# Key projection in seven block products from batch 2 on, and a first pass with the norm in halves and the row twice in PSUM

## The chip, the core and the metric

The kernel runs on one core of a Trainium2 chip. The time is that of the whole program on the device, in microseconds (us). TensorE (PE in the profile) multiplies matrices: a weight load (PEld) puts one operand into the array, the other streams through it, and the result goes to PSUM, a small memory of eight banks. VectorE (DVE), ScalarE (ACT) and GpSimd (POOL) do the rest, and SyncE (SP) issues most transfers (DMA). Each engine works through its own queue in order, and waits where an input isn't there yet or a buffer isn't free yet.

## The reference

The input x has 16 batches of 1024 nodes with 256 channels; adj is 1024 x 1024, and everything is float32. Two layers, each added to x:

```
h = relu(layernorm(x))
# layer 0
diff = mean over channels of h: column minus row
A    = 2 * | |sigmoid(diff) - 0.5| - 0.5 |
g    = relu( (h^T @ (adj * A_s)) * para )      A_s: A made symmetric
q    = g^T in 4 heads;   k, v = h @ kv_w
x    = x + softmax(q k^T * scale) @ v
# layer 1
h    = relu(layernorm(x))
agg  = A_hat @ h                               A_hat: adj + 1, normalized by its degrees
x    = x + batchnorm(relu(batchnorm(agg @ W1^T + b1)) @ W2^T + b2)
```

The two batch norms run over all batches and nodes, so that layer 1 ends only after a pass over everything.

## The kernel before

**The stages of a batch.** For each batch b the program records, in this order: `attention(b)`, `graph(b + 1)` and `linear1_all(b)`. Under a manual schedule the engines keep the order in which the instructions are recorded, and tiles take buffers from pools: a new tile takes the buffer that has been free longest, and its first writer waits until the old tile's last reader is done. In PSUM the pool `ps_s` has three buffers of two banks (tag "s"), and `ps_o` and `ps_t` have one bank each.

**`graph(b, between)`** (line 308) multiplies h with the weighted adjacency, chunk by chunk of 128 nodes: per chunk c four products of 128x512, into two PSUM tiles `f_gps`. A table `between` says what the other engines are given ahead of each chunk. Then come the keys (line 343): for each half d of the channels, two column halves g and two input halves e, so eight products of 128x512, in two PSUM tiles `f_kps`, each copied by ACT into kT (line 350). Behind each half DVE multiplies `f_gps` with para into qT (line 352) and ACT applies the ReLU and the scale (line 353). Then come the values (line 358), 16 products of 128x256, in two PSUM tiles `f_vps`, copied by ACT into v (line 365). Keys and values read hT, the transposed h.

**hT** is made by `turn_h` (line 288): DVE transposes blocks of 32 into two tiles `f_hQ` (tag "acc", two buffers), and 32 small transfers (line 302) put them in place; they are issued by POOL, in the first batch by SP.

**`linear1`** (line 550) and `linear1_seven` (line 648) already form their block products with seven instead of eight multiplications: a product of 2x2 blocks is written as seven products of sums of blocks. Four of the seven go into one PSUM tile one after another, and ACT copies what stands in it after each of them.

**Norm.** A `Norm` (line 206) takes statistics of 8 chunks of 128x256 on DVE (lines 221, 223), inverts the root of the variance on POOL (line 227), forms a shift on DVE (line 231), and applies norm and ReLU on ACT (line 236), which also sums each row for the mean over channels.

**The first pass.** Nothing runs beside batch 0's preparation, so its order is written out from line 878 on: the norm of batch 0, with two of the eight turns of adj (`turn_adj`: eight transposes on PE, and a copy into ahatT on ACT or DVE, lines 824 and 825) between its statistics and its activations; two more turns; `prepare_row(0)` (line 258: the column factor on DVE, the row of sums spread over all partitions by eight transposes on PE and copied out by ACT); then `weights` (line 275) per chunk: Abs and Tanh on ACT and a product with adj on DVE. The other turns, the turn of W1, the statistics of batch 1 and the row sums of adj stand in the table of `graph(0)`.

Of the kernel before, what the change touches and what calls it, by code (L numbers as in the profile page):

```python
# [29 lines left out]
def fast_path(  # L30
# [36 lines left out]
    w1s_d = dram.tile([P, 4, FC * P // 2], F32, tag="fw1s", name="fw1s")  # L67
    t_d = [dram.tile([P, 4, 512], F32, tag=f"ft_{k}", name=f"ft_{k}") for k in range(3)]
# [101 lines left out]
    with ExitStack() as stage:  # L170
# [12 lines left out]
        def load_x(b):  # L183
            xt = big.tile([P, NC, C], F32, tag="x", name=f"f_x_{b}")
            nc.sync.dma_start(xt, x[b].rearrange("(c p) d -> p c d", p=P))
            return xt


        xs, xr = {0: load_x(0)}, {}
# [16 lines left out]
        class Norm:  # L206
# [11 lines left out]

            def stats(self, c0, c1):
# [5 lines left out]
            def invert(self):  # L225
                nc.vector.tensor_scalar_add(self.var, self.mv[:, :, 1], EPS)
                nc.gpsimd.tensor_tensor(self.rstd, self.var, mhalf, ALU.pow)

            def relu(self, c0, c1):
                if c0 == 0:  # L230
                    nc.vector.scalar_tensor_tensor(  # L231
                        self.shift, self.mv[:, :, 0], -1.0, self.rstd, ALU.mult, ALU.mult
                    )
                    self.h = two.tile([P, NC, C], F32, tag="h", name=f"f_h_{self.name}")
# [23 lines left out]
        def prepare_row(b):  # L258
# [14 lines left out]
            nc.scalar.copy(row, ps.rearrange("p c q -> p (c q)"))  # L273
# [34 lines left out]
        def graph(b, between):  # L308
# [5 lines left out]
            for c in range(NC):  # L314
                for step in between.get(c, ()):
                    step()
                if c == 5:
                    for d in range(CC):
                        t = w4.tile([P, N], F32, tag="w4", name=f"f_para_{b}_{d}")
                        nc.sync.dma_start(t, para_v[:, d, :])  # L320
                        para_t.append(t)
                w = ws.pop((b, c))
                for d in range(CC):
                    for g in range(NH):
                        nc.tensor.matmul(  # L325
                            gps[d][:, ts(g, 512)],
                            hs[b][:, c, ts(d, P)],
                            w[:, ts(g, 512)],
                            start=(c == 0),
                            stop=(c == NC - 1),  # L330
                        )
# [7 lines left out]
            for d in range(CC):  # L339
                ps = ps_s.tile([P, N], F32, tag="s", name=f"f_kps_{b}_{d}")  # L340
                for g in range(NH):
                    for e in range(CC):
                        nc.tensor.matmul(  # L343
                            ps[:, ts(g, 512)],
                            kvw_t[:, e, ts(d, P)],
                            hT[e][:, ts(g, 512)],
                            start=(e == 0),
                            stop=(e == CC - 1),
                        )
                nc.scalar.copy(kT[:, d, :], ps)  # L350
# [3 lines left out]
            for c4 in range(0, NC, 4):  # L354
                ps = ps_s.tile([P, 4, C], F32, tag="s", name=f"f_vps_{b}_{c4}")
                for i in range(4):
                    for e in range(CC):
                        nc.tensor.matmul(  # L358
                            ps[:, i, :],
                            hT[e][:, ts(c4 + i, P)],  # L360
                            kvw_t[:, e, C : 2 * C],
                            start=(e == 0),
                            stop=(e == CC - 1),
                        )
                nc.scalar.copy(v[:, c4 : c4 + 4, :], ps)
# [276 lines left out]

        def load_w1_sums(b):
# [177 lines left out]
        def turn_adj(i, copy):  # L821
# [1057 lines left out]
```

## Time and profile before

| | us |
|---|---|
| time, median of three runs | 2459.4 (2456.1 to 2460.28) |
| the profiled execution | 2456.69 |
| its span, first to last instruction | 2454.9 |
| PE busy | 2399.2 (98%) |
| DVE busy | 1693.8 (69%) |
| ACT busy | 1319.9 (54%) |
| key products (line 343), all batches | 113.2 |
| value products (line 358), all batches | 113.1 |
| graph products (line 325), all batches | 444.7 |

A line of a group reads: line of the kernel, engine, operation, tile written <- tiles read, shapes, count | busy us, mean ns of one | idle time of that engine just before, and what ended it. A float32 matmul of the program appears as two records. The chain that ended last follows the work back from the last instruction, at each step to what released it; its lines are start, duration (us), and what ran. Times within a trace count from the start of the span.

### The profile page before, as it was taken

Reading aid. Unit: us, or ns where it says so; the run is one execution under the profiler, and the core shown is the slowest. Engines: PE = TensorE matmul, PEld = TensorE weight load, DVE = VectorE, ACT = ScalarE, POOL = GpSimd, SP = SyncE. Lnnn points to the kernel's source line nnn. Section 1 sums busy time; section 2 is a strip of 40 time slices with the busy share of each in tenths; the row PEclk is TensorE's granted clock in tenths of the full one; section 3 lists DMA queues with packets and bytes.
Section 4 is the critical chain, followed back from the end, with each engine's and each line's share of the span. In section 5 each row is a group of like instructions: output and inputs, shape, how many; then the busy total and the mean of one; then the engine's idle time right before and its main releaser. Section 6 shows DMA issues by size and latency. Waiting matters only on the chain.

```text
span 2454.9 us, 24503 instructions
## 1 busy us (share of the span) xinstructions
PE 2399.2 (98%) x8070; PEld 1060.6 (43%) x8070; DVE 1693.8 (69%) x2309; ACT 1319.9 (54%) x1896; POOL 307.8 (13%) x545
## 2 busy tenths in 40 slices
PE   7999999999999999999999999999999999999995
PEld 4443444434343434444343434343444434434444
DVE  4787668584949486776859494957668586747746
ACT  7746546464636455554546364646546465346643
POOL 2030202020020302020201102030202020000000
PEclk9999999999999999999999999999999999999998
DMA  5041414222331414142323223141414211455569
GB/s 180 5 142 61 146 61 124 82 84 71 113 93 60 139 61 146 60 138 69 115 61 105 81 82 115 64 142 61 146 60 122 84 39 57 134 201 171 170 214 371
DMA packets 174424, 271.81 MB, mean 111 GB/s; under 512 B 37585, under 2 KB 121041, under 8 KB 174289
## 3 DMA queue, kind: packets, MB, share of 16 engines
q1 hardware_dynamic: 154128, 237.62, 30.0%
q0 software_dynamic: 15552, 15.77, 2.5%
q10 hardware_dynamic: 4608, 16.78, 1.7%
q8 instruction: 66, 1.08, 0.2%
q14 instruction: 70, 0.57, 0.1%
HBM read 165.68 MB, written 70.84 MB: 96 GB/s over the span
## 4 chain that ended last, share of the span: by engine, by line
PE 94%; DVE 2%; DMA 2%; ACT 1%; issue 1%; POOL 0%; ACTq 0%; SPq 0%; DVEq 0%; POOLq 0%
PE f_s L379 18%; PE f_o L420 18%; PE f_gps L325 17%; PE f_aps L568 15%; PE f_zps L663 6%; PE f_vps L358 5%; PE f_kps L343 4%; PE f_zx L1092 3%; PE f_zm L1092 2%; PE f_z2ps L1030 2%; DVE f_x1t L1358 1%; PE f_zps L744 1%; PE f_zps3b L663 0%; PE f_zps3a L663 0%; ACT f_h_a L236 0%
## 5 line engine op out<-in xcount | busy, mean ns | idle before, releaser
L387 ACT ACTIVATE f_p<-f_s 128x1024 f32<-128x1024 f32 x512 | 477.4, 1046 | 153.4 <-PE f_s L379 153.2
L396 DVE TENSOR_TENSOR f_acc<-f_acc,f_p 128x1024 f32<-128x1024 f32 x384 | 470.4, 1225 | 42.1 <-DVE f_acc L396 1.4
L379 PE MATMUL f_s<-f_qT,f_kT 64*128 64x512 f32 x2048 | 456.9, 596 | 0.0
L420 PE MATMUL f_o<-f_p,f_v 128*64 128x512 f32 x2048 | 453.6, 595 | 0.0
L325 PE MATMUL f_gps<-f_w,f_h_a 128*128 128x512 f32 x1024 | 444.7, 594 | 3.8 <-DVE f_w L283 3.8
L302 POOL DMA_DIRECT2D f_hT<-f_hQ x480 | 235.7, 499 | 1219.1 <-PE f_gps L325 1088.4
L379 PEld LDWEIGHTS f_s<-f_qT,f_kT 64*128 64x128 f32 x2048 | 190.6, 185 | 263.5 <-ACT f_p L387 117.3
L325 PEld LDWEIGHTS f_gps<-f_w,f_h_a 128*128 128x128 f32 x1024 | 192.8, 190 | 251.9 <-issue 228.6
L420 PEld LDWEIGHTS f_o<-f_p,f_v 128*64 128x64 f32 x2048 | 141.4, 137 | 304.4 <-issue 255.6
L283 DVE SCALAR_TENSOR_TENSOR f_w<-f_w,f_adj 128x1024 f32<-128x1024 f32 x128 | 155.0, 1212 | 52.4 <-ACT f_w L282 52.4
L279 ACT ACTIVATE f_w<-f_row,f_col 128x1024 f32<-128x1024 f32 x128 | 148.2, 1157 | 27.2 <-DMA f_row<-frow 22.6
L236 ACT ACTIVATE f_h_b<-f_x,f_shift_b,f_rstd_b 128x256 f32<-128x256 f32 x128 | 64.6, 587 | 158.5 <-DVE f_shift_b L231 158.5
L611 DVE TENSOR_TENSOR f_aggT<-f_u,f_aps 128x512 f32<-128x512 f32 x16 | 11.0, 687 | 185.5 <-PE f_aps L568 185.5
L282 ACT ACTIVATE f_w<-f_w 128x1024 f32<-128x1024 f32 x128 | 135.4, 1058 | 4.1
L568 PE MATMUL f_aps<-f_ahatT,f_hs 128*128 128x512 f32 x256 | 115.1, 592 | 0.0
L343 PE MATMUL f_kps<-f_hT,f_kvw 128*128 128x512 f32 x256 | 113.2, 593 | 1.5 <-DVE f_qT L352 1.5
L568 PE MATMUL f_aps<-f_t,f_hs 128*128 128x512 f32 x256 | 112.5, 592 | 1.5 <-DVE f_hs L562 1.5
L358 PE MATMUL f_vps<-f_kvw,f_hT 128*128 128x256 f32 x512 | 113.1, 379 | 0.0
L568 PE MATMUL f_aps<-f_ahatT,f_h_b 128*128 128x512 f32 x256 | 112.6, 593 | 0.0
L358 PEld LDWEIGHTS f_vps<-f_kvw,f_hT 128*128 128x128 f32 x512 | 97.3, 190 | 20.1 <-issue 6.2
L236 ACT ACTIVATE f_h_a<-f_x,f_shift_a,f_rstd_a 128x256 f32<-128x256 f32 x128 | 75.0, 587 | 54.4 <-DVE f_shift_a L231 54.4
L393 DVE TENSOR_TENSOR f_acc<-f_p,f_p 128x1024 f32<-128x1024 f32 x64 | 76.2, 1191 | 30.7 <-ACT f_p L387 30.7
(187 smaller groups left out, 2554.7 us busy)
## 6 DMA issues: line engine op xcount, KB each, us to landing
f_t<-ft SPq DMA_DIRECT2D x84, 512.0 KB, 7.6
f_x<-in_x_dram SPq DMA_DIRECT2D x32, 1024.0 KB, 5.6
fz<-f_z SPq DMA_DIRECT2D x64, 512.0 KB, 9.4
f_zb<-fz SPq DMA_DIRECT2D x36, 512.0 KB, 4.2
f_para<-in_L_gnn_para_dram SPq DMA_DIRECT2D x32, 512.0 KB, 4.7
f_att<-f_oT SPq DMA_DIRECT2D x512, 32.0 KB, 1.9
fx<-f_x SPq DMA_DIRECT2D x16, 1024.0 KB, 5.9
f_x1t<-fx SPq DMA_DIRECT2D x32, 512.0 KB, 6.3
```

Source lines behind the costliest of these rows:

```text
L279: nc.scalar.activation(w, rows[b], AF.Abs, bias=cols[b][:, c : c + 1], scale=0.5 / C)
L283: nc.vector.scalar_tensor_tensor(w, w, 1.0, adj_t[c], ALU.subtract, ALU.mult)
L302: queue.dma_start(to[ts(k, 32), ts(a, 32 * NC)], t[ts(a, 32), k].rearrange("i c r -> i (c r)"),)
L325: nc.tensor.matmul(gps[d][:, ts(g, 512)], hs[b][:, c, ts(d, P)], w[:, ts(g, 512)], start=(c == 0), stop=(c == NC - 1),)
L343: nc.tensor.matmul(ps[:, ts(g, 512)], kvw_t[:, e, ts(d, P)], hT[e][:, ts(g, 512)], start=(e == 0), stop=(e == CC - 1),)
L358: nc.tensor.matmul(ps[:, i, :], hT[e][:, ts(c4 + i, P)], kvw_t[:, e, C : 2 * C], start=(e == 0), stop=(e == CC - 1),)
L379: nc.tensor.matmul(ps[:, e, :], kT[rows_e, pair, ts(m, P)], qT[rows_e, pair, ts(g, 512)], start=True, stop=True,)
L387: nc.scalar.activation(p, ps, AF.Exp)
L396: nc.vector.tensor_add(acc_of[s], acc_of[s], p)
L420: nc.tensor.matmul(o_of[s][e * HD : (e + 1) * HD, :], v[:, m, ts(2 * pair + e, HD)], p[:, e, :], start=(m == 0), stop=(m == NC - 1),)
L568: nc.tensor.matmul(ps, left[:, m, :], right(m), start=not more and m == 0, stop=(m == KH - 1), skip_group_check=more,)
L663: nc.tensor.matmul(ps[i], left[:, ts(i, P)], right, start=not more, stop=True, skip_group_check=more,)
```

## The change

Two parts of the kernel are changed.

*Keys.* For batches 2 to 15 the eight key products become seven products of 128x512. The four sums of blocks of the key weights are made once (`make_key_sums`, after the first graph), stored to memory, and loaded in each of these batches, ahead of chunk 6, into the second half of a tile of tag "acc". In `graph` the queries now come first, then DVE forms three sums t3, t2, t4 of blocks of hT, then come the values, then a fourth sum t1 in place, then the seven products: four into one PSUM tile x of tag "s", one into another of tag "s", and one each into `ps_t` and `ps_o`. ACT copies x after each of the four, and DVE adds the other three (one of them twice). Batches 0 and 1 keep the eight products.

*First pass.* The first x arrives in four transfers. The norm of batch 0 runs in two halves, its last two chunks are normalized by DVE instead of ACT. The row of sums is spread twice in PSUM: from the first copy ACT makes the first weights directly, in two halves of 512, and the second is copied out by DVE. The graph products of chunk 0 go through both channel halves for the first 512 columns, then for the others. The turns of adj are distributed anew: one ahead of the row, two ahead of the first product, the others in the table of `graph(0)`, every second one of the later ones through the banks of `ps_o` and `ps_t`; DVE copies seven of the eight out, ACT one. The norm of batch 1 moves from chunk 4 to chunk 6, weights 7 from chunk 5 to chunk 4, and the sums of W1 from chunk 5 to behind the graph.

```diff
-        def load_x(b):
+        def load_x(b, step=NC):
             xt = big.tile([P, NC, C], F32, tag="x", name=f"f_x_{b}")
-            nc.sync.dma_start(xt, x[b].rearrange("(c p) d -> p c d", p=P))
+            from_x = x[b].rearrange("(c p) d -> p c d", p=P)
+            for c in range(0, NC, step):
+                nc.sync.dma_start(xt[:, c : c + step, :], from_x[:, c : c + step, :])
             return xt
-        xs, xr = {0: load_x(0)}, {}
+        xs, xr = {0: load_x(0, 2)}, {}
...
+            def vector_relu(self, c0, c1):
+                self.place()
+                for c in range(c0, c1):
+                    nc.vector.tensor_scalar(
+                        self.h[:, c, :], self.xt[:, c, :], self.mv[:, c, 0:1],
+                        0.0, ALU.subtract, ALU.max,
+                    )
+            def vector_scale(self, c0, c1):
+                for c in range(c0, c1):
+                    nc.vector.tensor_scalar_mul(
+                        self.h[:, c, :], self.h[:, c, :], self.rstd[:, c : c + 1]
+                    )
+                nc.vector.tensor_reduce(
+                    self.sums[:, c0:c1], self.h[:, c0:c1, :], AX.X, ALU.add
+                )
...
-            nc.scalar.copy(row, ps.rearrange("p c q -> p (c q)"))
+            first = ps.rearrange("p c q -> p (c q)")
+            if b > 0:
+                nc.scalar.copy(row, first)
+                return
+            second = ps_s.tile([P, NC, P], F32, tag="s", name="f_rps2_0")
+            for c in range(NC):
+                nc.tensor.transpose(
+                    second[:, c, :], sums_of[0][:, c : c + 1].to_broadcast([P, P]), ident
+                )
+            w = w4.tile([P, N], F32, tag="w4", name="f_w_0_0")
+            for g in range(NH):
+                at = slice(512 * g, 512 * (g + 1))
+                nc.scalar.activation(
+                    w[:, at], first[:, at], AF.Abs, bias=cols[0][:, 0:1], scale=0.5 / C
+                )
+                nc.scalar.activation(w[:, at], w[:, at], AF.Tanh)
+            nc.vector.tensor_copy(row, second.rearrange("p c q -> p (c q)"))
+            for g in range(NH):
+                at = slice(512 * g, 512 * (g + 1))
+                nc.vector.scalar_tensor_tensor(
+                    w[:, at], w[:, at], 1.0, adj_t[0][:, at], ALU.subtract, ALU.mult
+                )
+            ws[0, 0] = w
...
+                if c == 6 and b > 1:
+                    t23 = pp.tile([P, 2, 512], F32, tag="acc", name=f"f_kt23_{b}", bufs=2)
+                    rest = pp.tile([P, 2, 512], F32, tag="acc", name=f"f_kt4_{b}", bufs=2)
+                    sums = rest[:, 1].rearrange("p (n q) -> p n q", n=4)
+                    nc.sync.dma_start(sums, kvs_d)
...
+            t2, t3, t4 = t23[:, 0], t23[:, 1], rest[:, 0]
+            part = lambda k, j: hT[k][:, ts(j, 512)]
+            a = lambda i, k: kvw_t[:, k, ts(i, P)]
+            for d in range(CC):
+                queries(d)
+            nc.vector.tensor_sub(t3, part(1, 1), part(0, 1))
+            nc.vector.tensor_add(t2, t3, part(0, 0))
+            nc.vector.tensor_sub(t4, part(1, 0), t2)
+            values()
+            t1 = part(0, 1)
+            nc.vector.tensor_sub(t1, t1, part(0, 0))
...
+            c = lambda i, j: kT[:, i, ts(j, 512)]
+            x = ps_s.tile([P, 512], F32, tag="s", name=f"f_kpsx_{b}")
+            m7 = ps_s.tile([P, 512], F32, tag="s", name=f"f_kps7_{b}")
+            m2 = ps_t.tile([P, 512], F32, tag="t", name=f"f_kps2_{b}")
+            m4 = ps_o.tile([P, 512], F32, tag="o", name=f"f_kps4_{b}")
+            mult(x, a(0, 0), part(0, 0))
+            nc.scalar.copy(c(0, 0), x)
+            mult(m2, a(0, 1), part(1, 0))
+            nc.vector.tensor_add(c(0, 0), c(0, 0), m2)
+            mult(x, sums[:, 1], t2, True)
+            nc.scalar.copy(c(1, 0), x)
+            mult(m7, sums[:, 2], t3)
+            nc.vector.tensor_add(c(1, 0), c(1, 0), m7)
+            mult(x, sums[:, 0], t1, True)
+            nc.scalar.copy(c(1, 1), x)
+            mult(m4, a(1, 1), t4)
+            nc.vector.tensor_add(c(1, 1), c(1, 1), m7)
+            nc.vector.tensor_add(c(1, 0), c(1, 0), m4)
+            mult(x, sums[:, 3], part(1, 1), True)
+            nc.scalar.copy(c(0, 1), x)
...
-            prepare_start(0)
-            for i in range(2):
-                turn_adj(i, nc.scalar.copy)
-            prepare_end(0)
+            norm.stats(0, HALF)
+            norm.invert(0, HALF)
+            norm.stats(HALF, BY_VECTOR)
+            norm.shifts(0, HALF)
+            norm.stats(BY_VECTOR, NC)
+            norm.invert(HALF, NC)
+            norm.vector_relu(BY_VECTOR, NC)
+            norm.relu(0, HALF, False)
+            norm.shifts(HALF, NC)
+            norm.relu(HALF, BY_VECTOR, False)
+            norm.vector_scale(BY_VECTOR, NC)
+            hs[0] = norm.h
+            turn_adj(0)
+            place_adj(0, nc.vector.tensor_copy)
             xs[1] = load_x(1)
-            for i in range(2, 4):
-                turn_adj(i, nc.vector.tensor_copy)
             prepare_row(0)
-            weights(0, 0)
-            for i in range(4, 6):
-                turn_adj(i, nc.vector.tensor_copy)
             weights(0, 1)
+            turn_adj(1)
+            turn_adj_aside(2)
+            place_adj(1, nc.vector.tensor_copy)
...
-                    1: [lambda: weights(0, 3), lambda: turn_adj(6, nc.scalar.copy)],
-                    2: [turn_w1, lambda: weights(0, 4), lambda: prepare_start(1)],
-                    3: [lambda: weights(0, 5), lambda: turn_adj(7, nc.scalar.copy)],
-                    4: [lambda: weights(0, 6), lambda: prepare_end(1), lambda: again(0)],
-                    5: [lambda: weights(0, 7), make_w1_sums],
+                    1: [
+                        lambda: weights(0, 3),
+                        lambda: place_adj_aside(2, nc.vector.tensor_copy),
+                        lambda: turn_adj(3),
+                        lambda: place_adj(3, nc.scalar.copy),
+                    ],
+                    2: [
+                        lambda: weights(0, 4),
+                        turn_w1,
+                        lambda: prepare_start(1),
+                        lambda: turn_adj_aside(4),
+                        lambda: place_adj_aside(4, nc.vector.tensor_copy),
+                    ],
+                    3: [
+                        lambda: weights(0, 5),
+                        lambda: turn_adj(5),
+                        lambda: place_adj(5, nc.vector.tensor_copy),
+                    ],
+                    4: [
+                        lambda: weights(0, 6),
+                        lambda: weights(0, 7),
+                        lambda: turn_adj_aside(6),
+                        lambda: place_adj_aside(6, nc.vector.tensor_copy),
+                    ],
+                    5: [
+                        lambda: turn_adj(7),
+                        lambda: place_adj(7, nc.vector.tensor_copy),
+                    ],
+                    6: [lambda: prepare_end(1), lambda: again(0)],
...
+            make_w1_sums()
+            make_key_sums()
             prepare_row(1)
```

## The prediction

> **What bounds the kernel now.** I read the page's shares first, then the chain that ended last, then PE's waits, then the stretches of PE, ACT and DVE around the two edited places. The profiled execution took 2456.69 us: a span of 2454.9 and 1.8 around it. Its page:
>
> ```profile
> PE 2399.2 (98%) x8070; PEld 1060.6 (43%) x8070; DVE 1693.8 (69%) x2309; ACT 1319.9 (54%) x1896; POOL 307.8 (13%) x545
> ...
> PE 94%; DVE 2%; DMA 2%; ACT 1%; issue 1%; POOL 0%; ACTq 0%; SPq 0%; DVEq 0%; POOLq 0%
> ...
> L343 PE MATMUL f_kps<-f_hT,f_kvw 128*128 128x512 f32 x256 | 113.2, 593 | 1.5 <-DVE f_qT L352 1.5
> ```
>
> TensorE is busy 98% of the span and 94% of the chain. Every 133.8 us the chain repeats for one batch with no gap. So a matmul taken out shortens the time by its place in the chain, and a wait put before one lengthens it. One 128x512 f32 product is two records (256 for 16 batches x 8 products). The chain through one batch gives the pitch:
>
> ```profile
> 1624.77 3.86 PE f_gps L325 x9
> 1628.63 6.87 PE f_kps L343 x16
> 1635.50 4.53 PE f_vps L358 x21
> ```
>
> 6.87/16 = 0.429 us per record, 0.859 per product. The start is the one place where PE waits. The chain there, in order of time:
>
> ```profile
> 10.41 0.04 issue
> 10.46 1.98 PE f_adjps L824 x8
> ...
> 13.37 4.79 ACT f_h_a L236 x16
> 18.16 0.04 issue
> 18.20 0.34 PE f_rps L270
> 18.54 0.02 issue
> 18.56 1.02 ACT f_row L273
> 19.59 0.02 issue
> 19.61 1.16 ACT f_w L279
> 20.77 0.02 issue
> 20.79 1.06 ACT f_w L282
> 21.86 0.02 issue
> 21.88 1.24 DVE f_w L283
> 23.11 0.04 issue
> 23.16 3.70 PE f_gps L325 x8
> ```
>
> Two copies of the adjacency on ACT, eight norm activations, the row copy and the first weights stand one behind the other until 23.16. The first keys start at 54.52, wait 1.5 us for the para load, and attention starts at 71.05.
>
> **Part 1, the keys of batches 2 to 15.** Eight products become seven: 14 batches x 0.859 = 12.0 us off the chain, if nothing new waits. Against it:
>
> (a) Three of the seven (the second, third and fourth into bank x) wait until ACT has copied what stands in x. One other product of 0.859 us lies in between. A copy takes 0.586 (128x512, L609). Its path: the last record ends 0.17 us after the next would start (593 ns against a pitch of 429), ACT starts 0.03 later (aps ends 575.05, copy starts 575.08), 0.59 copy, 0.04 to PE: 0.83. That fits by 0.03. But a weight load normally starts 0.24 ahead of its matmul, and it stands behind the wait. The only restart shown after such a wait (23.16) has a first record of 0.70 instead of 0.59, so 0.1 more: 0.07 us per wait. Bounds: 0 (the 0.03 fits) and 0.21 (all 0.24 lost). 42 waits: 2.9 us (0 to 8.8).
>
> (b) The first copy of x stands behind the norm activations, two ReLUs and two value copies on ACT. With T0 the end of the graph products, the second value copy can start at T0+7.06 (16 value products of 0.43, then the drain). ACT is there in time when the norm ends before T0+4.24: ReLU 0.92, ReLU 0.97, copy 0.92 follow. Over 14 batches it ends at T0+3.5 to 4.3, except here, where T0 is 1628.63 and the norm ends at 1633.77, T0+5.14:
>
> ```profile
> 1629.83 4.04 ACT L236 ACTIVATE f_h_b<-f_x,f_shift_b,f_rstd_b 128x256 f32<-128x256 f32 x8 [11.44 <-DVE f_shift_b L231]
> ```
>
> 0.9 us for that batch (0 to 2: such a batch may not occur, or twice).
>
> (c) DVE gets eight 128x512 operations of 0.69 (L561): 5.5 us per batch, beside the 11.6 us it idles there per batch (L611: 185.5 us over 16). Behind them stand the four sums of the first linear layer. They are ready at about T0+15.2 and PE wants the second at T0+6.87+6.01+6.87 = T0+19.7; without these 4.5 us PE would wait in the third product of that layer. ACT: two copies of 1.00 become four of 0.586, +0.34 us, in idle time.
>
> (d) One more load on SP per batch, 256 KB, behind the para loads. Its slot is that of the first half of the turned rows, free before para is issued, so the store of x behind it isn't held up. In the late batch para is issued at 1622.9; a 512 KB load takes 4.2 to 7.6 us to land on this page, so the sums are there by about 1632, and the product that reads them comes at T0+8.6 = 1637.2. Cost 0; with that cover gone, the lateness itself, per batch.
>
> (e) The first product of the linear layer behind the keys takes a PSUM buffer that the values used, not bank x: no wait for the last copy.
>
> Sum of part 1: -12.0 + 2.9 + 0.9 = -8.2 us (bounds -12.0 and -1.2).
>
> **Part 2, the first pass.** Four x loads instead of one (each issued in at most 0.45 us on SP, ahead of adj) let DVE start its statistics before 6.29. The first rstd can't start before POOL has issued its six column loads (6.22). A pow over 8 columns takes 1.68, over 2 0.70: about 1.03 for 4. First rstd 7.3, four ACT activations from 7.6 (0.585 each); second rstd 9.7; two more activations to 11.2, while DVE makes the last two chunks (two plain operations on 128x256, at most 0.42 each, before the rstd, two behind it, and a reduce of 0.7): sums at 11.3 instead of 18.16. Then DVE copies adj 0 (1.2) ahead of the column factor: 12.7. ACT turns the row in PSUM into the first weights in halves (four of about 0.57): 15.0. The second row copy ends on DVE at 14.8, the halves at 15.5 and 16.2. PE meanwhile turns the row twice and adj 1 and 2, 32 transposes, before the first product. Eight took 1.94 us at 8.19, sixteen 1.91 at 18.36, so 3.8 to 7.8 us from 11.5; taking 0.2 for the first half: 16.5. First product 16.5 (15.5 to 19.3) instead of 23.16.
>
> From there PE has 8 x 3.44 for the graph and six groups of eight transposes at 0.87 (adj 3 to 7 and W1; before there were three): 32.7, keys at 49.2 against 54.52. ACT's weights take 2.13 per chunk against PE's 3.44, and DVE's seven adj copies (1.2 each) stay ahead of the next turn into the same bank. SP's 32 transfers for the turned rows (21.2 us, L302) start at 22 instead of 28.8, para goes right behind them at 43.2 and lands at 48.6 (5.34 before), so the wait of 1.5 goes. Behind para now: x of batch 0 and the two sums, wanted much later. ACT's norm of batch 1 waits for DVE's last adj copy (40), and with the eight row sums ends at 53.4: the first key copy then starts 0.4 us late, hidden by the second keys. Attention at 64.3 instead of 71.05: -6.8. For restarts between the six groups (0.1 each, as at 23.16) I take off 0.6: -6.2 us. Bounds: -7.8 (first product at 15.5) and -2.3 (at 19.3, and two first products at twice their time, 1.7, as the transposes show a factor of two).
>
> The slow transposes stand at a granted clock of 1.00, as the fast ones do, so the row says nothing of the reason. [...] In the trace the first graph products behind transposes and 2.9 us of idle ran at 0.44 a record, full rate; I go by that.
>
> **Sum.** -8.2 - 6.2 = -14.4: 2456.69 becomes 2442.3. The three runs shown have a median 2.7 above the profiled execution (2456.1 to 2460.28), so against the median: 2445.0.
>
> **Rivals.**
> 1. The copies eat part 1: waits of 0.86 per batch, so only the first pass is left: 2459.4 - 6.2 = 2453. For it: the 0.03 us of room in (a). Against: even the upper bound of (a) is 0.63 per batch.
> 2. Part 1 works, the first pass doesn't: PE's cold transposes, the three added turns before the keys, or ACT's row sums take it back: 2459.4 - 8.2 = 2451. For it: six groups of transposes stand behind the first product instead of three, 2.6 us. Against: 6.7 us earlier start.
> 3. All waits fit, both parts in full: 2459.4 - 12.0 - 7.8 = 2440.
> 4. Slower: ACT becomes the bound at bank x. Its work before the first copy is 7.9 us (4.04 + 0.92 + 0.97 + 2 x 1.0) of the 8.6 that PE leaves. From 1.3 us of wait per batch (18.2/14) all gain is gone; at 2 us per batch: 28 - 18.2, 2469. For it: the batch with 0.9. Against: one batch of 14 only, and the norm's start, set by DVE's shift, isn't moved.
> That the change removes no matmul can't be: the order lists seven products for each of batches 2 to 15.
>
> **How the numbers follow.** Forecast (2441 to 2450) 0.60; rival 1 0.10; rival 2 0.10; rival 3 0.13; rival 4 0.07. About 0.2% (4.9 us) can be told from no change. Rival 1 and 2 at their slow edge give the same: 0.07 together; slower 0.05, as rival 4 at its weak edge is within the bound; faster 0.88. The range: rival 3 on the profiled execution, 2437, up to 2453, which takes in rivals 1 and 2 at their centres.
>
> **What would show it.** Key products at 14 records per batch, 6.0 us plus gaps below 0.3; PE waiting for ACT's copy of bank x by some 0.1 us, three times a batch; vps straight behind the graph products; no wait of the first linear products; in the first pass, the first graph product near 16.5, keys near 49, attention near 64. Wrong if the gaps in the keys near 0.86 a batch, if the sums' load or DVE's added work appears in PE's waits, or if attention starts later than 68.

## The result, and the profile after

The changed kernel takes 2446.91 us (median of five runs, 2445.7 to 2447.76), the kernel before 2459.4 (2456.1 to 2460.72). The ratio is 0.995, with a 95% interval of 0.994 to 0.9961. The forecast was 2445.0 in a range of 2437 to 2453.

The profiled execution of the changed kernel took 2446.91 us, with a span of 2445.0. The one of before took 2456.69, so profile against profile the gain is 9.8 us, where my sum had 14.4. That comparison, not the one of the medians, tests the steps. From the page of the changed kernel, the busy times and the shares of the chain that ended last:

```profile
PE 2390.1 (98%) x8050; PEld 1052.2 (43%) x8050; DVE 1777.3 (73%) x2440; ACT 1316.7 (54%) x1918; POOL 308.2 (13%) x546
...
PE 79%; DVE 11%; SPq 3%; DMA 3%; ACT 2%; issue 2%; POOL 1%; DVEq 0%; ACTq 0%; POOLq 0%
```

TensorE has 9.1 us less to do. The chain now leaves it in places: through DVE, the SP queue and ACT, where it was 94% TensorE before; TensorE is still busy 98% of the span, so these shares say where work is handed over and not how much time is lost there. Four landmarks (start of an operation on TensorE, us from the start of the span) say where the gain lies:

| | before | after | gain so far |
|---|---|---|---|
| first scores of batch 0 | 70.98 | 65.64 | 5.3 |
| graph products of batch 2 | 262.17 | 256.68 | 5.5 |
| first scores of batch 15 | 2043.82 | 2033.57 | 10.25 |
| end of the span | 2454.9 | 2445.0 | 9.9 |

The first pass gave 5.5, the keys of batches 2 to 15 gave 10.25 - 5.5 = 4.8. The chain through the values and keys of batch 4, start and duration, where before had `f_kps` 6.87 and then `f_vps` (4.53 in the chain shown with the prediction, cut off by its window):

```profile
550.97 6.91 PE f_vps L423 x32
557.88 0.86 PE f_kpsx L464 x2
558.74 0.86 PE f_kps L464 x2
559.60 1.00 PE f_kpsx L464 x2
560.60 0.86 PE f_kps L464 x2
561.45 0.94 PE f_kpsx L464 x2
562.40 0.86 PE f_kps L464 x2
563.26 0.94 PE f_kpsx L464 x2
564.20 2.15 PE f_aps L690 x5
```

The keys take 6.32 instead of 6.87. The second, third and fourth product into bank x take 1.00, 0.94 and 0.94 instead of 0.86. The weight loads of the same stretch (start, duration; in brackets the idle time of the load path and what ended it) show why:

```profile
558.58 0.19 PEld L464 LDWEIGHTS f_kps<-f_hT,f_kvw 128*128 128x128 f32 x1 [0.24 <-issue]
559.47 0.30 PEld L464 LDWEIGHTS f_kpsx<-f_kt,f_kt 128*128 128x128 f32 x2 [0.70 <-ACT f_kT L474]
...
561.27 0.30 PEld L464 LDWEIGHTS f_kpsx<-f_hT,f_kt 128*128 128x128 f32 x2 [0.65 <-ACT f_kT L478]
```

The first load stands for the undisturbed case: one load per 0.43 us, each a whole record (0.43 us) ahead of the record that uses it; the 0.24 in its brackets is the idle time between two loads. The loads for bank x started only when ACT's copy was done (559.42), at 559.47, where the product itself starts too: both loads of the product then come in its own time, 0.30 for two, and its second record starts about 0.1 late.

In four of the 14 batches the first copy itself comes late. The list of waits (total, times, longest) and the chain through batch 7:

```profile
PE f_kpsx L464 <- ACT f_kT L474: 2.9, 4, 0.9
```

```profile
944.37 2.19 DMA f_att<-f_oT
...
946.73 1.24 DVE f_x L614
...
950.03 1.67 POOL f_rstd_b L257
...
951.93 4.04 ACT f_h_b L278 x8
955.97 1.90 ACT f_qT L416 x2
957.86 1.80 ACT f_v L430 x2
959.66 0.49 ACT f_kT L474
...
960.20 1.12 PE f_kpsx L464 x2
```

This is the path of my step (b): the norm of the batch ends late, ReLUs and value copies stand behind it on ACT, then the copy. In batch 7 the chain leads back to the attention's output, 32 KB pieces that SP issues one by one: one issue took 2.10 us where the others took 0.59. In batch 12 it is the last piece, which landed 4.0 us after its issue (median 2.0). Batch 8 has another cause. Its pieces landed on time and the variance was ready at 1082.76, but POOL made the inverse root only from 1084.36, behind a transfer of the turned rows that it had to issue first:

```profile
1083.84 0.50 POOL L368 DMA_DIRECT2D f_hT<-f_hQ  x1 [1.08 <-DMA f_hT<-f_hQ]
1084.36 1.66 POOL L257 TENSOR_TENSOR f_rstd_b<-f_var_b,f_mhalf 128x8 f32<-128x8 f32 x1
```

### The profile page after: what moved, and what is told of

It is laid out like the page before. It is cut to its first block, busy times and chain, and to the rows that moved or that the text cites. A ratio compares the mean times of both kernels' runs of the same rounds, so it can differ in the third digit from the quotient of the medians.

```text
span 2445.0 us, 24677 instructions
## 1 busy us (share of the span) xinstructions
PE 2390.1 (98%) x8050; PEld 1052.2 (43%) x8050; DVE 1777.3 (73%) x2440; ACT 1316.7 (54%) x1918; POOL 308.2 (13%) x546
## 4 chain that ended last, share of the span: by engine, by line
PE 79%; DVE 11%; SPq 3%; DMA 3%; ACT 2%; issue 2%; POOL 1%; DVEq 0%; ACTq 0%; POOLq 0%
PE f_aps L690 15%; PE f_s L501 14%; PE f_o L542 14%; PE f_gps L398 13%; PE f_zps L796 5%; DVE f_acc L518 3%; PE f_vps L423 3%; PE f_zx L1283 3%; SPq L606 3%; PE f_zm L1283 2%; PE f_kpsx L464 2%; PE f_z2ps L1221 2%; PE f_kps L464 1%; ACT f_h_b L278 1%; DVE f_w L349 1%
## 5 line engine op out<-in xcount | busy, mean ns | idle before, releaser
L584 ACT COPY f_recs<-f_rec 32x32 f32<-32x32 f32 x128 | 31.5, 246 | 98.6 <-DVE f_rec L576 97.5
L569 ACT COPY f_parts<-f_red 32x64 f32<-32x64 f32 x128 | 39.1, 305 | 78.4 <-DVE f_red L534 77.3
```

## The experiments

Every kernel was timed against the kernel before in five rounds. "T0" is where the graph products of a batch end on TensorE (the start of the next product in the timeline; the chain puts it some 0.2 later); the first linear product comes 13.23 later in an undisturbed batch of the changed kernel, 13.77 with eight key products.

### e1 and e2: each part alone

```diff
 e1: the first pass of the kernel before; make_key_sums() behind graph(0); keys as changed
 e2:
-            if b < 2:
+            if True:
                 for d in range(CC):          # eight products in every batch
...
-            make_key_sums()
```

> The kernel before with the seven key products of batches 2 to 15 alone; the first pass is that of before. If the two parts are independent, as my sum assumed, this run gives what the landmarks of the changed kernel give for the keys, 4.8 us under before (graph products of batch 2 to scores of batch 15: 10.24 less 5.49): about 2454.6, and the three products that wait show 1.00, 0.94 and 0.94 us as there. Rival: the late batches of the changed kernel (2.9 us) come from the first pass having moved the phase of the DMA queues; then the norm ends early here as in before, at most one batch waits, and this run is 7 to 8 us under before.

> The changed first pass with eight key products in every batch and no sums of the key weights. Expected 5.3 to 5.5 us under before (attention of batch 0 at 65.71 instead of 71.05): about 2454. If the head start were lost again on the way to the end (as 1.3 us are at the start of the second stage of the changed kernel), 4 us. e1 and e2 together should make 10 to 11, as against 12.5 of both at once by the medians.

Measured: e1 2454.1 (ratio 0.9978, 0.9969 to 0.9987), e2 2450.67 (0.9966, 0.9954 to 0.9978), before beside them 2458.81. So 4.7 and 8.1 under before, 12.8 together; both at once gave 12.5. The two parts add, as far as the intervals tell. (Profile against profile e2 gives 5.6; the rest of its 8.1 is that the median of before lies above its profiled execution.)

The rival of e1 falls: it has late batches too, without the changed first pass (8, 12 and 14; in batch 8 the first linear product came at T0+16.19). They are older than the change: in the kernel before the norm of batch 12 ended at T0+5.41 and cost nothing, and in e2 that of batch 8 at T0+6.42 and cost 0.7, since there only the copies of whole key and value tiles stand behind it. The change took that cover away: 5.48 costs it 1.05 in batch 8. Which batches are late differs from kernel to kernel: the keys waited in 7, 8, 12 and 13 in the changed kernel, in 8, 12 and 14 in e1.

e2 gave more than the changed kernel's own landmarks: attention at 64.64 against 65.64. The first pass varies by more than I had allowed for, as five kernels with the same first pass show:

| | adj 0 turned at | transposes at full rate from | second row copied from | first graph product | first scores of batch 0 |
|---|---|---|---|---|---|
| changed kernel | 10.27 | 15.2 | 15.51 | 17.48 | 65.64 |
| e4 | 9.96 | 15.2 | 15.36 | 17.33 | 65.48 |
| e3 | 9.43 | 15.0 | 14.82 | 16.79 | 64.94 |
| e5 | 9.49 | 13.5 | 14.29 | 16.25 | 64.52 |
| e2 | 9.71 | 12.7 | 13.97 | 15.94 | 64.64 |

In each of them TensorE starts its transposes 0.21 us apart, and 0.11 apart from the time in the third column on. That time and the landing of adj 0 set when the second row is in PSUM; DVE copies it, and the first product follows 1.97 us after the start of that copy in all five.

The profile of the changed kernel is the late end; the mean gain at the attention of batch 0 is 5.9 against the one profile of before. The first pass of before varies too: e1, which has it, reached the same point at 72.40 instead of 70.98.

### e3: the ReLUs of the queries behind the keys

```diff
             for d in range(CC):
-                queries(d)                       # multiply and ReLU
+                nc.vector.tensor_mul(qT[:, d, :], gps[d], para_t[d])
...
             nc.scalar.copy(c(0, 1), x)
+            for d in range(CC):
+                query_relu(d)
```

> The changed kernel with the two ReLUs of the queries (0.92 and 0.97 us on ACT) moved from ahead of the first copy of bank x to behind the last one. Theory: the first copy is late in some batches because ACT has norm, two ReLUs and two value copies in a row; 1.9 us less ahead of it moves the limit of the norm's end from T0+4.24 to T0+6.1, later than any batch shows (T0+5.5). Then the waits of 2.9 us go, the three restarts of 0.14, 0.09 and 0.09 per batch stay, and it is 2.5 to 3 us under the changed kernel, about 2444. Rival: the late batches are a transfer's doing that PE waits for elsewhere too; then the loss stays or moves and the time is that of the changed kernel, 2447.

Measured: 2445.43 (0.9942, 0.9929 to 0.9956), 1.5 under the changed kernel; by the spans 2.6, of which 0.7 is an earlier first pass (table above). The waits for the first copy are gone from the list, though the norm ended at T0+5.09 in batch 7 and T0+6.38 in batch 8: the first linear products came at 13.22 and 13.37. The undisturbed batch still took 13.22, so the restarts stayed, as the theory had it. One new wait took back 1.6, in the last batch, where no linear layer stands between the keys and the scores:

```profile
PE f_s L507 <- ACT f_qT L420: 1.6, 1, 1.6
```

### e4 and e5: value products between the key products

```diff
-            values()
+            for i in range(4):
+                value(4, i)                      # rows 512 to 1023 first: t1 overwrites them
             t1 = part(0, 1)
...
             mult(x, a(0, 0), part(0, 0))
             nc.scalar.copy(c(0, 0), x)
+            value_copy(4)
             mult(m2, a(0, 1), part(1, 0))
+            value(0, 0)
             mult(x, sums[:, 1], t2, True)
             nc.scalar.copy(c(1, 0), x)
             mult(m7, sums[:, 2], t3)
+            value(0, 1)
             mult(x, sums[:, 0], t1, True)
...
 e5, on top of e4:
-            xm = ps_s.tile([P, 2, 512], F32, tag="s", name=f"f_kpsx_{b}")
-            x, m7 = xm[:, 0], xm[:, 1]
+            x = ps_s.tile([P, 512], F32, tag="s", name=f"f_kpsx_{b}")
-            m4 = ps_o.tile([P, 512], F32, tag="o", name=f"f_kps4_{b}")
+            m7 = ps_o.tile([P, 512], F32, tag="o", name=f"f_kps7_{b}")
...
+            m4 = ps_t.tile([P, 512], F32, tag="t", name=f"f_kps4_{b}")
...
-                for a in range(4):               # turn_h: order of the transfers
+                for a in (2, 3, 0, 1) if b > 1 else range(4):
```

Both kernels also have the ReLUs of the queries later on ACT, as e3 has: one behind the third copy of x, one behind the fourth.

> The changed kernel with the value products of the second four row blocks first, and one value block (two products of 0.43) put between each pair of key products as more cover for the copies of bank x: 1.72 us of PE work instead of 0.86 stand between a product into x and the next one. The ReLUs of the queries stand later on ACT, the seventh product in the other bank of x's buffer. Theory: a restart costs only when the wait is still open at the time when the weights would be loaded ahead. Then all products take 0.86, the 4.3 us of restarts and the 2.9 us of late batches both go: 7 us under the changed kernel, 2440. Rival: any accumulating product behind a wait on ACT starts 0.1 late, whether or not the copy has long been done; then 0.3 per batch stays, only the late batches are won, 2444.

> As the interleaved kernel before it (e4), with its two side effects taken away: the second product that stands by itself has a bank of its own instead of the second half of x's buffer (there it waited 0.68 for the copy of the first half, 14 times), and the transfers that turn the rows send the second half first, since the values now begin with it (there the first value products waited 0.65). Theory: weights that can be loaded ahead make every key product 0.86, so that keys and values take 12.9 us per batch instead of 13.23, and the late batches are covered up to a norm that ends at T0+5.4: 2.9 + 4.8 us under the changed kernel's span, 2439 to 2440. Rival: a product behind a satisfied wait on ACT still starts 0.1 late: 13.2 per batch, 2443 to 2444.

e4 measured 2457.34 (0.9996, 0.9987 to 1.0005): neither theory's number, and 10.4 over the changed kernel. Both losses are of my own making. From TensorE's timeline, batch 4:

```profile
553.27 1.97 PE L469 MATMUL f_vps<-f_kvw,f_hT 128*128 128x256 f32 x8 [0.39 <-issue]
555.50 1.53 PE L469 MATMUL f_vps<-f_kvw,f_hT 128*128 128x256 f32 x6 [0.26 <-DMA f_hT<-f_hQ]
...
561.15 1.13 PE L486 MATMUL f_kpsx<-f_kt,f_kt 128*128 128x512 f32 x2 [0.68 <-ACT f_kT L502]
```

The values now began with the rows that arrive last, which made TensorE wait in batch 4 and two more. And the standalone product m7, put into the second half of x's tile, waited for ACT's copy of the first half: 9.5 us in 14 batches. Waits follow the tile here, not the half that is touched. An undisturbed batch has its first linear product at T0+14.04.

e5, with both mended, measured 2440.08 (0.9929, 0.9915 to 0.9942): 6.8 under the changed kernel, as the theory had it. Its batch 4:

```profile
552.52 1.02 PE L486 MATMUL f_kpsx<-f_hT,f_kvw 128*128 128x512 f32 x2
553.38 1.02 PE L486 MATMUL f_kps<-f_hT,f_kvw 128*128 128x512 f32 x2
554.24 1.03 PE L469 MATMUL f_vps<-f_kvw,f_hT 128*128 128x256 f32 x4
555.10 1.02 PE L486 MATMUL f_kpsx<-f_kt,f_kt 128*128 128x512 f32 x2
555.96 1.02 PE L486 MATMUL f_kps<-f_kt,f_kt 128*128 128x512 f32 x2
```

Read the starts: 0.86 apart throughout, into x as elsewhere, and the first linear product comes at T0+12.91 (13.18 in the one late batch, 8). From the graph products of batch 2 to the scores of batch 15 e5 takes 1769.4 us, the changed kernel 1776.9 (the landmarks above), 7.5 less: about all of the 4.3 + 2.9 that the two kinds of wait cost. That the late batches no longer count may be due to the values in between or to the later ReLUs, which alone had done it in e3; the restarts, which stayed in e3, went with the values. The same instructions with the same dependencies took 0.86 where the copy was done early. The restart, 0.09 to 0.14 in the changed kernel, was the price of a wait that was still open when the weights could have been loaded, not of the wait as such: the rival falls.

### e6 and e7: the row ahead of the adjacency

```diff
-            turn_adj(0)
-            place_adj(0, nc.vector.tensor_copy)
             xs[1] = load_x(1)
             prepare_row(0)
...
+            turn_h(0, nc.sync)
             weights(0, 1)
(and: turns of adj 0 and 1 behind chunk 0, one more behind each later chunk;
 prepare_end(1) at chunk 5; first half of w ahead of the row copy)
...
 e7: e5 with this
```

> The changed kernel with only its first pass altered: PE turns the row twice before any tile of the adjacency, the first two tiles are turned behind the first chunk's products, DVE makes the first half of the weights before the row copy and turns h before the second chunk's weights, and ACT has the norm of batch 1 ahead of the last tiles. Theory: in the changed kernel the first product is late because PE and then DVE serve the adjacency tile that lands at 10.13 ahead of the row. Then the row is in PSUM at about 12.4 instead of 13.92 and the first product stands at 14.5 to 15.5 instead of 17.48; keys at 48 to 49, 2 to 3 us under the changed kernel, 2444. Rival: TensorE is slow at its start (0.24 a transpose against 0.12) whatever stands first; then the row's 16 transposes end no earlier than 13.9, or the first products themselves run at half their rate, and less than 1 us is won.

> e5 and e6 together. The two act in different places, so their gains should add: 2436 to 2438 if both theories hold, the better of the two alone if one falls.

e6 measured 2445.73 (0.9955, 0.9941 to 0.9968), e7 2441.02 (0.9933, 0.992 to 0.9947): no gain over the changed kernel and over e5 that can be told from none. The start of e6 on TensorE:

```profile
9.06 2.23 PE L312 MATMUL f_rps<-f_ident,f_sums 128*128 128x128 f32 x4 [9.06 <-ACT f_h_a L278]
11.47 1.48 PE L312 MATMUL f_rps<-f_ident,f_sums 128*128 128x128 f32 x4 [0.18 <-ACT f_h_a L278]
12.75 1.91 PE L323 MATMUL f_rps<-f_ident,f_sums 128*128 128x128 f32 x8
15.12 4.74 PE L399 MATMUL f_gps<-f_w,f_h_a 128*128 128x512 f32 x8 [0.46 <-DVE f_w L337]
```

The first product came at 15.12, 2.4 earlier, as the theory said. But the keys came at 51.60 instead of 50.90. Two things ate it. The three turns of adj that stood ahead of the first product, 2.6 us at full rate, now stand behind it. And the first eight graph records took 4.74 instead of 3.67: the slow start of TensorE, which transposes had paid in the changed kernel (0.21 us apart instead of 0.11), was paid by products here, three records of 0.86 instead of 0.43. Both the theory on the start and its rival on the rate were true; the start of the first product was the wrong thing to aim at, since TensorE has work to do from the landing of adj 0 on.

### e8 to e10: is TensorE slow at its start because it has not worked yet?

```diff
 e8 (on e5):
             nc.vector.tensor_scalar_mul(cols[b], sums_of[b], -0.5 / C)
+            if b == 0:
+                place_adj(0, nc.vector.tensor_copy)
...
-            place_adj(0, nc.vector.tensor_copy)
 e9 (on e8), first instructions of TensorE:
+            warm = ps_t.tile([P, 512], F32, tag="t", name="f_warm")
+            for n in range(16):
+                nc.tensor.matmul(warm[:, :P], ident, ident, start=True, stop=True)
 e10 (on e8):
+            for n in range(26):
+                nc.tensor.transpose(warm[:, :P], ident, ident)
```

> The second interleaved kernel (e5) with one step moved in the first pass: DVE makes the column factor ahead of the copy of the first adjacency tile. It is the control for the two kernels below. The row's transposes still end at 13.9 (two times eight at 0.24 from 10.27), so ACT's first weights still start at about 14.0 and nothing is won: 2440, the first product at 17.0 to 17.5. If DVE's copy and not PE held the first weights, 0.5 to 1 us is won.

> The same as e8 with 16 products of the identity by itself on TensorE from 2.7 us on, when it has nothing else to do; their result is not used. In e6 the first three graph records took 0.86 each instead of 0.43, at a granted clock of 1.00, and turned to full rate 5.8 us after TensorE's work began; in the changed kernel the transposes turned from 0.24 to 0.12 after 5.0 us. Theory: TensorE is slow by a factor of two for some 5 us of its own work, whatever the work is, and the first pass pays for it. Then the transposes from 10.3 on take 0.12, the row is in PSUM at 12.5 instead of 13.9, the first product stands at 15.3 to 15.7 instead of 17.5, 1.8 to 2.2 us under e8, about 2438. Rival: the slowness ends at a fixed time after the start of the program (15.3 in the changed kernel, 15.1 to 17.5 in e6), or is that of transposes whose inputs have just been written; then the time is that of e8.

> As e9, with 26 transposes of the identity instead of the products. If any work of TensorE counts, the time and the first product are those of e9. If only products count, the transposes from 10.3 on still take 0.24 and the time is that of e8.

Measured: e8 2439.1 (0.9924, 0.991 to 0.9937), e9 2440.28 (0.9925, 0.9911 to 0.9938), e10 2439.8 (0.992, 0.9907 to 0.9934). The times of the three can't be told apart, nor from e5's, but the traces can. In e8 the first product came at 16.60 (16.25 in e5): the column factor had held nothing up. TensorE in e9:

```profile
2.69 5.66 PE L1065 MATMUL f_warm<-f_ident 128*128 128x128 f32 x32 [2.69 <-POOL f_ident masks.py:199]
9.59 1.09 PE L989 MATMUL f_adjps<-f_ident,f_adj 128*128 128x128 f32 x8 [1.24 <-DMA f_adj<-in_adj_dram]
...
15.36 3.67 PE L400 MATMUL f_gps<-f_w,f_h_a 128*128 128x512 f32 x8
19.68 1.10 PE L989 MATMUL f_adjps<-f_ident,f_adj 128*128 128x128 f32 x8 [0.65 <-DVE f_ahatT L995]
...
25.40 1.07 PE L1059 MATMUL f_w1ps<-f_ident,f_w1n 128*128 128x128 f32 x8 [1.18 <-DMA f_w1n<-in_L_gnn_W_dram]
```

The identity's records stood 0.21 us apart up to 6.5 and 0.11 behind it. Eight transposes at 9.59 took 1.09 instead of 1.94, and the first product came at 15.36 instead of 16.60 in e8: behind other work of TensorE the same transposes ran at full rate, which no run without such work had before 12.7 (e2), so the slowness was not that of a time or of the transposes. But two waits, 0.65 (0.30 in e8) for DVE's copy of adj 1 and a new one of 1.18 for the landing of W1, took it back: the first scores stand at 65.14 against 64.75 in e8.

In e10 the transposes of the identity went the same way: they started 0.21 us apart from 2.69 up to 6.2 and 0.11 apart from 6.3 on. Then came 2.42 us of idle time. The stretches of 2 us (length, busy PE, PEld, DVE, ACT, POOL, then the granted clock):

```profile
8.00:10.00 2.00, 0.13 (x1) 0.13 (x2) 1.75 (x10) 1.78 (x7) 0.65 (x1) 0.91 1.05 299
10.00:12.00 2.00, 2.00 (x10) 2.00 (x11) 1.42 (x5) 1.91 (x7) 0.40 (x1) 0.50 1.02 369
12.00:14.00 2.00, 2.00 (x16) 2.00 (x15) 1.26 (x2) 0.60 (x1) 0.00 (x0) 0.74 1.02 410
```

The granted clock fell to 0.50 in the stretch from 10 to 12, and the transposes stood 0.21 apart again. So e10 does not separate "only products count" by its time; its first rows do, against it.

### e11 and e12: take the two waits of e9 away

```diff
                     1: [
                         lambda: weights(0, 3),
                         lambda: place_adj_aside(2, nc.vector.tensor_copy),
-                        lambda: turn_adj(3), ...
                     ],
-                    2: [..., turn_w1, ...]
+                    2: [..., lambda: turn_adj(3), ..., lambda: turn_adj_aside(4), ...],
+                    3: [lambda: weights(0, 5), turn_w1],
 e11: with the 16 products of e9; e12: without
```

> e9 with the later turns in another order, since e9's gain of 1.24 us at the first product was lost again to two waits of TensorE: 0.65 for the place that the fourth adjacency tile takes and 1.18 for the landing of the first layer's weights. The second chunk's products now stand straight behind the first's, the fourth tile and the fifth behind these, and the first layer's weights are turned one chunk later, where they have landed. Theory: the two waits go and the start made earlier reaches the attention of batch 0: 63.3 instead of 65.14 in e9 and 64.75 in e8, so 1.4 us under e8, 2437.7. Rival: the next one late takes their place (ACT's row sums, which end near 56, in front of the first key copies, or the load of the query weights behind the turned rows) and the attention stays at 64.5 or later.

> e11 without the 16 products at the start: the control for them. The transposes take 0.24 again, the first product stands at 16.5 as in e8; only the waits of 0.26 and 0.30 of e8 can go: attention at 64.4, so 1.1 us above e11, 2438.8.

Measured: e11 2440.72 (0.9927, 0.9913 to 0.994), e12 2439.93 (0.9925, 0.9912 to 0.9939). The two waits are gone, and the rival was right, with another culprit than I had named. In e11:

```profile
24.72 0.66 PE L1004 MATMUL f_adjpsa<-f_ident,f_adj 128*128 128x128 f32 x4 [1.46 <-DVE f_ahatT L1010]
```

The fifth tile waits for the banks that DVE has yet to empty of the third. First scores at 64.66 in e11 and 65.50 in e12: in these traces the 16 products at the start win 0.84 of the 1.1 expected and the new order loses 0.75 against e8. Together they move the attention of batch 0 by 0.1, within what one run differs from the next, and the times of the three can't be told apart.

## Why the prediction was right, and where it was off

The time, 2446.91 for 2445.0, lies in the range, and both parts work as the change says. By the steps, profile against profile, 4.6 of the 14.4 us are missing:

| step | predicted | measured | shown by |
|---|---|---|---|
| keys, one product less | -12.0 | -12.0 | e5: all products at 0.86 |
| (a) restarts at bank x | +2.9 (0 to 8.8) | +4.3 | chain after; e3, e5 |
| (b) late first copy | +0.9 (0 to 2) | +2.9 | list of waits after; e3, e5 |
| (c) DVE, (d) load of the sums, (e) bank of the linear layer | 0 | 0 | no such wait after |
| first pass | -6.2 (-7.8 to -2.3) | -5.5 | landmarks; e2 |
| second stage and output | 0 | +0.4 | landmarks |

Point by point:

*(a)* The mechanism was right and the size off. I took 0.1 for a restart and set the room of 0.03 against it, so 0.07 per wait. All three waits of a batch restart: 0.14, 0.09 and 0.09, so 14 x 0.31 = 4.3. The copy was done at 559.42, 0.01 before the product would have started; such room is none for a weight load that starts 0.43 ahead elsewhere (I had taken the 0.24 of idle time between two loads for that lead). 42 restarts of 0.1, with nothing set against them, would have been 4.2.

*(b)* The place was right, the count wrong. The limit, T0+4.24 in the chain's times, is T0+4.43 in the timeline's, and norms that end later delay the keys one for one: 5.32, 5.48, 5.50 and 4.81 in the four batches made the first linear product 0.88, 1.05, 1.06 and 0.37 late. That is 3.4 in all: 2.9 of waiting and a restart of 0.1 behind each wait. The sum of the table closes at 4.8 all the same, since before lost 0.5 of its own in the keys of batches 4 and 8. I had counted one late batch of 14 in one trace of another kernel, and even there batches 9 and 14 ended at T0+4.55 and T0+4.49, just past the limit. The changed kernel has four and e1 three. There is one trace of each, so whether the kernel or the execution decides is not shown; 8 or 12 is among the late ones in most. The bound of 2 us, "twice", was a count of one stretched by one. Rival 4 named this mechanism with the right point of decision; it costs 0.2 a batch, far from its 1.3.

*(c), (d), (e)* hold: the linear layer waits once for its sums, 1.3 us, where before did so for 1.5, and nothing waits for the load of the key sums.

*First pass.* The first product came 1.0 later than in my sum, by another path. I let adj 0 be turned well before the row; x in four pieces is issued ahead of it, it landed at 10.13 instead of 8.1, and TensorE served it ahead of the row. Then DVE's copy of the second row stood ahead of the first weights:

```profile
10.27 1.94 PE L957 MATMUL f_adjps<-f_ident,f_adj 128*128 128x128 f32 x8 [10.27 <-DMA f_adj<-in_adj_dram]
12.00 1.92 PE L312 MATMUL f_rps<-f_ident,f_sums 128*128 128x128 f32 x8
13.71 1.77 PE L323 MATMUL f_rps<-f_ident,f_sums 128*128 128x128 f32 x8
15.51 1.22 DVE L333 COPY f_row<-f_rps 128x1024 f32<-128x1024 f32 x1 [1.96 <-PE f_rps L323]
...
17.48 3.67 PE L398 MATMUL f_gps<-f_w,f_h_a 128*128 128x512 f32 x8 [0.26 <-DVE f_w L336]
```

I had that copy end at 14.8; it began at 15.51, when the second row was in PSUM, and ended at 16.73, then the first half of the weights was made. The column factor (13.39 instead of 12.7) and the four half activations (0.66 instead of 0.57 each) were late too, but ACT started on the first row only when that was in PSUM, and e8, with the column factor earlier, won nothing. In the other four kernels of the table the first product came between 15.94 and 17.33, so that 16.5 lies in the middle is luck of where adj 0 and the doubling of the rate fall. The keys came at 50.90 where I had 49.2: 1.0 of the difference is the later start, the rest waits (0.31 for DVE's copy of adj 1) and restarts. The wait for the para load is gone, as said.

*The slow start.* TensorE's transposes stood 0.21 us apart, twice the later 0.11, for 3.0 to 6.2 us from its first record on (e2 9.71 to 12.7, changed kernel 10.27 to 15.2, before 8.19 to 14.4, e9, with products, 2.69 to 6.5), and e6, where products of the graph came earlier, had them at half rate (0.86 a record), up to about 17.2 and so 8 us behind its first record, with waits in between. Transposes alone were followed by the full rate too: in the changed kernel and in e10 nothing else ran before the rate doubled, and the changed kernel's first products came at full rate (eight records in 3.67). I went by the trace of before, where 2.9 us of idle time stood ahead of the first products and eight records took 3.70. For this change that was the right guide; for e6 it was not, its eight records took 4.74. And that start was one outcome of two: e1 has the same start and the other outcome (last section).

*Where the gain went by medians.* 12.5 against 14.4. The kernel before has a median 2.7 over its profiled execution, the changed kernel none, so the miss of 4.6 shows as 1.9. That is luck of one profiled run, and not a merit of the sum. Of the runs of before that stand beside the experiments, those with a granted clock of 0.996 took 2457.6 on average and those with 0.993 2459.2, so part of its spread goes with the clock; where in the span isn't shown.

## What to carry to other kernels

A matmul that waited on a copy lost its weight load's head start of 0.43 us even where the copy was done in time for the matmul itself (by 0.01 in batch 4), and came 0.09 to 0.14 late. Here 0.86 us of other work between was not enough for a copy of 0.59, and 1.72 was, as e5 had it by weaving the values into the keys; what would do between the two wasn't tried. It recovered what the waits had cost: e5 and the kernels built on it, e7 to e12, take 2439.1 to 2441.0 us and can't be told from one another; the changed kernel's fastest run took 2445.7. When a stage is reordered, ask what hid the lateness that is already there: a norm that ended at T0+5.4 cost nothing while eight key products stood there (before, batch 12), and 1.06 after the change (batch 12 again, T0+5.5). And in a start-up where every engine feeds the next, an earlier first product is no gain by itself: e6, e9 and e11 each moved it by 1.2 to 2.4 us, and no time of the program followed: e6 met the slow rate and the turns that it had put off, e9 and e11 the next wait.

## What the runs showed of the hardware

*Behind the same idle time TensorE ran slow in one run and at full rate in another.* The kernel before and e1 share their first pass, with 2.89 us of idle time ahead of the first graph product in both. Before, the eight records took 3.70; in e1 they took 5.40:

```profile
23.28 5.40 PE L395 MATMUL f_gps<-f_w,f_h_a 128*128 128x512 f32 x8 [2.89 <-DVE f_w L348]
```

In the stretch from 24 to 26 the granted clock was 0.50 there and 1.00 before. That is the bound of 1.7 us that I had set on slow first products, met in a run of the other part. In e10 the granted clock was 0.50 behind 2.42 us of idle time; behind 1.24 in e9 it stayed at 1.00, and eight transposes took 1.09. What decides is not settled by these runs.

*The granted clock did not show the slow start.* It stands at 1.00 in every stretch from 8 to 18 us of the changed kernel, while transposes started 0.21 apart up to 15.2 and 0.11 apart from there on. In e1 and e10 the fall after work shows as 0.50. Here the durations were the safer guide.
